# The last 512 queries' output in two parts: three pairs of heads early, the last pair at the end

## The chip, the core and the metric

The kernel runs on one NeuronCore of a Trainium2 chip. The metric is the device time of one execution in microseconds (us). The engines are TensorE (PE in the profile, PEld for its weight loads), VectorE (DVE), ScalarE (ACT), GpSimd (POOL) and SyncE (SP), which here only issues DMAs.

## What is computed

Four sequences (B = 4) of 1024 tokens with 256 channels go through four residual blocks: a linear recurrence, a sparse feed-forward block, attention, and the feed-forward block again. Two of them matter here.

```python
x = x + attention(layernorm(x))     # 8 heads of 64, softmax over 1024 keys, out @ Wo.T
x = x + ffn(layernorm(x))
# ffn, for each of two branches:
#   xc = grouped convolution of x;  mean and var of xc over ALL 4096 tokens
#   score = softmax(linear(gelu(normalised xc)));  the 32 largest of 256 are kept
```

The mean and variance run over all tokens of all sequences. The second feed-forward block can therefore not compute a single score before the attention output of the last token is in x and its convolution has been measured.

## The kernel before

Tokens are worked on in tiles of 128; x stays on the chip as 32 tiles. `heads` computes attention for one sequence: it loops over two halves of 512 queries (`nb`), four pairs of heads (`g`, PAIRS = 4) and four tiles of 128 queries (`q`). One such unit makes, for each of its two heads (`j`), the scores `sc` by four matmuls (L881), the negated maximum `nm` on VectorE (L885), and the exponentials `pr` on ScalarE (L889). The exponentials must be transposed, and there are two ways:

- by DMA (`by_dma`, q = 0 and 2): ScalarE casts `pr` to 16 bits (L892), GpSimd makes the remainder (L893), and SyncE issues a transposing DMA into `d` (L894);
- by TensorE (q = 1 and 3): eight transposes into PSUM (`ptp`, L900), copied out by VectorE and ScalarE (L903, L905).

`values_sum` then multiplies the transposed exponentials with the values (`pmo`, L925: 48 matmuls after a DMA, 32 after TensorE), puts the reciprocal sums in place with one transpose (L933), copies those on ScalarE (`rb`, L935) and multiplies on VectorE into `on` (L936). These sums are held back: the list `pending` holds units by TensorE and is taken from in the next unit, `late` holds units by DMA and is taken from in the next unit by DMA, and what is left follows after the loops.

`output` makes the projection of one query tile. It splits `on` (128 x 512: four pairs of 128) into a high part on ScalarE (`onp0`, L945) and a low part on GpSimd (`onp1`, L946), multiplies both with the split weights (`products`, three matmuls per pair, so twelve per tile into `pmy`, L170) and adds the result to x on VectorE (L948). `onp0` and `onp1` have one buffer each.

`f2.head` is the start of the second feed-forward block for two tiles of a block (its argument `pairs` says which two): layer norm on VectorE (L133 to L136, `rsqrt` being L55 to L66), normalisation on ScalarE (`xn`, L145), transposes (`pt`, L147), a copy (`ft`, L524), the convolution (`pc`, L529), an activation (`xc_f`, L533) and the statistics (`bst_f`, L534). When all statistics are there, `norm_scale` turns them into a scale, and the 32 tiles of the feed-forward block follow (`Ffn.tile`: maxima and replacements at L674, the subtraction of line 628, and so on).

`merge` interleaves all of this: `heads` is the main list of steps (STEPS = 64 per sequence), and each entry of `side` is (step at which it starts, generator, steps between its parts). A scheduler then orders each engine's queue by its own estimate of times. The queues are in order: an instruction that waits holds up all behind it on its engine. For the last sequence the output of the second half of queries starts a step before the end with two tiles, then comes the head of the feed-forward block for these, and after the merge the other two tiles and their head.

Of the kernel before, what the change touches and what calls it, by code (L numbers as in the profile page):

```python
# [10 lines left out]
F32 = mybir.dt.float32  # L11
I32 = mybir.dt.int32
F32R = mybir.dt.float32r
# [3 lines left out]
ALU = mybir.AluOpType  # L17
# [4 lines left out]
P = 128  # L22
B = 4
# [5 lines left out]
NBLK = B * T // 512  # L29
HEADS = 8  # L30
HD = 64
PAIRS = HEADS // 2
# [132 lines left out]
def products(nc, dst, pairs, start=True, stop=True):  # L165


    terms = [(x, y) for a, b in pairs for x, y in ((a[0], b[0]), (a[0], b[1]), (a[1], b[0]))]
    for i, (x, y) in enumerate(terms):
        nc.tensor.matmul(dst, x, y, start=start and i == 0, stop=stop and i == len(terms) - 1)  # L170


def by_block(v):

    return [
        v[b * T : (b + 1) * T, :].rearrange("(q p r) d -> r p q d", p=P, r=CH)[r] for b in range(B) for r in range(CH)
    ]
# [12 lines left out]
STEPS = 64  # L190
# [4 lines left out]
class Lru:  # L195
# [31 lines left out]
    def two(self, name):  # L227
        return [self.cp.tile([P, KD, D], F32R, tag=f"{name}{i}", name=f"{name}{i}") for i in range(2)]
# [544 lines left out]
class Attention:  # L773
# [82 lines left out]
    def heads(self, b, psum):  # L856

        nc, sp, wp = self.nc, self.sp, self.hp  # L860
        kh, kl, la, lb = self.k[b]
        late, pending = [], []
        for nb, g, q in ((nb, g, q) for nb in range(2) for g in range(PAIRS) for q in range(4)):
            by_dma = q % 2 == 0
            if g == 0:
                self.on[b, nb, q] = wp.tile([P, PAIRS, P], F32, tag=f"on{q}", name=f"on{q}")
            qs = self.qs[b, nb, g]
            ssum = sp.tile([P, 2], F32, tag="ssum", name="ssum", bufs=4)
            if by_dma:
                pts = [wp.tile([P, 2 * TPB, P], F16, tag=f"d{j}", name=f"d{j}", bufs=2) for j in range(2)]  # L870
                parts = ((0, lb[0]), (TPB, lb[0]), (0, lb[1]))
                terms = [(v[:, c, :], i + c) for c in range(TPB) for i, v in parts]
            else:
                pts = [wp.tile([P, TPB, P], F32, tag=f"p{j}", name=f"p{j}") for j in range(2)]
                terms = [(la[:, c, :], c) for c in range(TPB)]
            for j in range(2):
                sc = psum.tile([P, T], "sc", "sc")
                for i, kk in enumerate((kh, kl)):
                    for kb in range(2):
                        sl = slice(kb * 512, (kb + 1) * 512)  # L880
                        nc.tensor.matmul(  # L881
                            sc[:, sl], qs[:, j, q * P : (q + 1) * P], kk[:, sl], start=(i == 0), stop=(i == 1)
                        )
                nm = sp.tile([P, 1], F32, tag="nm", name="nm", bufs=4)
                nc.vector.tensor_reduce(nm, sc, AX.X, ALU.max, negate=True)  # L885
                if by_dma:
                    nc.vector.tensor_scalar(nm, nm, PSHIFT * math.log(2.0), None, ALU.add)  # L887
                pr = wp.tile([P, T], F32, tag="pr", name="pr", bufs=3)
                nc.scalar.activation(pr, sc, AF.Exp, bias=nm, accum_out=ssum[:, j : j + 1])  # L889
                if by_dma:  # L890
                    pd = wp.tile([P, 2, T], F16, tag="pd", name="pd", bufs=2)
                    nc.scalar.copy(pd[:, 0, :], pr)  # L892
                    nc.gpsimd.tensor_tensor(pd[:, 1, :], pr, pd[:, 0, :], ALU.subtract)  # L893
                    nc.sync.dma_start_transpose(pts[j], pd.rearrange("p i k -> p (i k)"))  # L894
                else:
                    for half in range(2):
                        pt = psum.tile([P, 4, P], "t", "ptp")
                        for kk in range(4):
                            kc = 4 * half + kk
                            nc.tensor.transpose(pt[:, kk, :], pr[:, kc * P : (kc + 1) * P], self.ident)  # L900
                        dst = pts[j][:, 4 * half : 4 * half + 4, :]
                        if half == 0 and b == B - 1:
                            nc.vector.tensor_copy(dst, pt)  # L903
                        else:
                            nc.scalar.copy(dst, pt)  # L905
                if j == 0 and pending:
                    self.values_sum(*pending.pop(0), psum)
                if j == 1 and late and by_dma:
                    self.values_sum(*late.pop(0), psum)
                yield  # L910
            (late if by_dma else pending).append((pts, terms, ssum, self.on[b, nb, q][:, g, :]))
        for args in late + pending:
            self.values_sum(*args, psum)
# [21 lines left out]
        nc.scalar.copy(rb, po[:, 1, :])  # L935
        nc.vector.tensor_tensor(on, po[:, 0, :], rb, ALU.mult)  # L936

    def output(self, b, nb, psum, tiles=range(4)):

        nc = self.nc  # L940
        for q in tiles:
            xt = self.x[b * TPB + nb * 4 + q]
            py = psum.tile([P, D], "s", "pmy")
            on = [self.hp.tile([P, PAIRS, P], F32R, tag=f"onp{i}", name=f"onp{i}") for i in range(2)]
            nc.scalar.copy(on[0], self.on[b, nb, q])  # L945
            nc.gpsimd.tensor_tensor(on[1], self.on[b, nb, q], on[0].bitcast(F32), ALU.subtract)  # L946
            products(nc, py, [([t[:, g, :] for t in on], [t[:, g, :] for t in self.wvo]) for g in range(PAIRS)])
            nc.vector.tensor_tensor(xt, xt, py, ALU.add)  # L948
            yield

# [23 lines left out]
def run(*gens):  # L974
    for g in gens:
        for _ in g:
            pass
# [51 lines left out]
def tile_kernel(ctx: ExitStack, tc: tile.TileContext, x_in, w_lru, vecs_in, rows, w_ffn, lin_t, w_attn, w_down, out):  # L1029
    nc = tc.nc  # L1030
# [31 lines left out]
    f2 = Ffn("f2", tc, bp, x, w)  # L1062

    with ExitStack() as c1:
        psum = Banks(c1.enter_context(tc.tile_pool(name="ps1", space=PSUM)), {"pu": 2, "po": 2, "py": 2, "pt": 2})
# [15 lines left out]
        for k in range(NBLK):  # L1081
            last = k >= NBLK - 2
# [10 lines left out]
            b = k // CH + 1  # L1093
# [24 lines left out]
    with ExitStack() as c2:  # L1118
        sp = c2.enter_context(tc.tile_pool(name="at_s", bufs=2))
        wp = c2.enter_context(tc.tile_pool(name="at_w", bufs=1))  # L1120
        two = lambda shape, name: [wp.tile(shape, F32R, tag=f"{name}{i}", name=f"{name}{i}") for i in range(2)]
        wqk, wvo, wd = two([P, KD, HEADS * HD], "wqk"), two([P, PAIRS, D], "wvo"), two([P, KD, P], "wd")
# [3 lines left out]
        at = Attention(tc, x, ident, ident64, wqk, wvo, wd, sp, wp)  # L1126
        with ExitStack() as c4:
            psum = Banks(
                c4.enter_context(tc.tile_pool(name="ps4", space=PSUM)), {"pl": 2, "px": 1, "pf": 2, "at": 3}
            )  # L1130
# [5 lines left out]
            with tc.issue_after(f1.gelu(1)):  # L1136
                for blk in range(2, NBLK):
                    g = f1.gelu(blk)
            with tc.issue_after(g):
                warm(nc, sp, AF.Exp)  # L1140
            tiles = [
                f1.tile(i, fp, psum, ("pl", "px", "pf"), fast=i == TPB - 1, tt=tts[i // 4]) for i in range(TPB)
            ]
# [24 lines left out]
        psum = Banks(c2.enter_context(tc.tile_pool(name="ps2", space=PSUM)), {"sc": 2, "t": 2, "s": 2})  # L1168
        at.hp = c2.enter_context(tc.tile_pool(name="at_h", bufs=1))
        fp = c2.enter_context(tc.tile_pool(name="f_s", bufs=2))  # L1170
        side = []
        for b in range(B):
            n = STEPS * b
            side += [
                (n + nb * 32 + 8 * g - 7, at.queries(b, nb, g, psum, "s"), 1)
                for nb in range(2)
                for g in range(PAIRS)
                if b or nb or g
            ]
            side.append((n + 33, at.output(b, 0, psum), 1.5))  # L1180
            side.append((n + STEPS - 1 if b == B - 1 else n + STEPS + 1.5, at.output(b, 1, psum, range(2 if b == B - 1 else 4)), 1 if b == B - 1 else 1.5))
            side.append((n + 40 if b == B - 1 else n + STEPS + 24, f2.head(2 * b, sp, psum, "s"), 2))
            last = b == B - 1
            side.append((n + STEPS if last else n + STEPS + 8, f2.head(2 * b + 1, sp, psum, "s", (0,) if last else (0, 1)), 1 if last else 2))
            if b < B - 1:
                side.append((n + 38, chain(at.prepare(b + 1, 0, psum, "s"), at.values(b + 1, 0, psum, "s")), 1.5))
                side.append((n + 56, chain(at.prepare(b + 1, 1, psum, "s"), at.values(b + 1, 1, psum, "s")), 1.5))
        side.append((1, at.values(0, 1, psum, "s"), 1))
        for i in range(TPB, NT):
            n = i - TPB  # L1190
            start = 1 + 6.75 * n if n < TPB else STEPS * (n // TPB) - STEPS + 48.25 + 8 * (n % TPB + 1)
            side.append((start, f1.tile(i, fp, psum, "sss", parts=wfs, fine=True), [1, 1, 1, 1, 1, 2, 1]))
        merge(chain(*(at.heads(b, psum) for b in range(B))), side)
        run(at.output(B - 1, 1, psum, range(2, 4)), f2.head(NBLK - 1, sp, psum, "s", (1,)))
    with ExitStack() as c3:
        psum = Banks(c3.enter_context(tc.tile_pool(name="ps3", space=PSUM)), {"pl": 2, "px": 3, "pf": 3})
        fp = c3.enter_context(tc.tile_pool(name="f_e", bufs=4))
# [5 lines left out]
        tiles = [f2.tile(i, fp, psum, ("pl", "px", "pf"), by_block(out), fast=i >= NT - 2) for i in range(NT)]  # L1203
# [98 lines left out]
```

## Time and profile before

| | us |
|---|---|
| median of 4 runs | 1535.94 |
| lowest and highest of the runs | 1532.78, 1540.67 |
| profiled execution | 1541.21 |
| its span, first to last instruction | 1539.5 |
| busy in the span: TensorE, VectorE, ScalarE, GpSimd | 1300.6, 1182.3, 1015.8, 682.2 |

In the profile's rows, a time stands first (start in us from the span's beginning, or a total), then the duration in us, the engine, the line, the operation and `out<-in`. `xN` means N instructions merged into one row; the bracket at the end tells how long the engine had been idle just before and what ended that. The windows view gives busy time of each engine in a stretch, with the number of instructions; PEclk is the share of the clock that TensorE was granted.

### The profile page before, as it was taken

How to read it: one execution, taken by the hardware profiler on the slowest of the kernel's cores; microseconds unless marked ns; L12 is line 12 of the kernel's file. 1: busy time of each engine (PE TensorE's matmuls, PEld its weight loads, DVE VectorE, ACT ScalarE, POOL GpSimd, SP SyncE). 2: the span in 40 equal slices, each digit the busy share in tenths (PEclk: the TensorE clock that was granted, in tenths of full speed). 3: DMA queues.
4: the chain of work that ended last, by engine and by line, in shares of the span. 5: the costliest groups of instructions: out<-in, count | busy, mean ns of one | idle time of the engine just before them, and what ended most of it. 6: DMA issues, size and time to landing. Idle time of an engine off the chain costs nothing. (4 is left out here: it accounts for less than half of the span.)

```text
span 1539.5 us, 28691 instructions
## 1 busy us (share of the span) xinstructions
PE 1300.6 (84%) x10134; PEld 963.8 (63%) x10136; DVE 1182.3 (77%) x3674; ACT 1015.8 (66%) x2145; POOL 682.2 (44%) x848
## 2 busy tenths in 40 slices
PE   5879998698898898888988989888999998656775
PEld 3535455365676766766776767677777776434454
DVE  8976665697878887878768687777676675499998
ACT  5353433664787877796777777877777776466664
POOL 2043423161545453544544544454344434057776
PEclk9999999698999999999999999999999999779898
DMA  3010000331454343334433444334444554000000
GB/s 117 32 41 14 21 21 14 134 105 41 76 97 89 63 76 73 73 73 82 81 73 60 71 78 82 64 61 82 71 82 80 87 95 85 1 11 27 22 25 28
DMA packets 288609, 96.51 MB, mean 63 GB/s; under 512 B 268233, under 2 KB 284626, under 8 KB 288466
## 3 DMA queue, kind: packets, MB, share of 16 engines
q1 hardware_dynamic: 283024, 88.50, 28.6%
q10 hardware_dynamic: 5442, 6.18, 1.2%
q8 instruction: 80, 1.31, 0.3%
q14 instruction: 63, 0.52, 0.1%
HBM read 16.01 MB, written 11.53 MB: 18 GB/s over the span
## 5 line engine op out<-in xcount | busy, mean ns | idle before, releaser
L893 POOL TENSOR_TENSOR pd<-pr,pd 128x1024 f16<-128x1024 f32 x128 | 273.5, 2142 | 256.3 <-ACT pd L892 196.7
L885 DVE TENSOR_REDUCE nm<-sc 128x1 f32<-128x1024 f32 x256 | 308.5, 1218 | 77.8 <-PE sc L881 76.1
L889 ACT ACTIVATE pr<-sc,nm 128x1024 f32<-128x1024 f32 x256 | 286.2, 1121 | 91.5 <-DVE nm L887 54.7
L881 PE MATMUL sc<-kh,qs 128*128 128x512 f32 x512 | 185.3, 440 | 28.1 <-ACT pr L889 20.4
L881 PE MATMUL sc<-kl,qs 128*128 128x512 f32 x512 | 161.6, 396 | 0.0
L674 DVE MATCH_REPLACE8 wk<-m,wk 128x256 f32<-128x256 f32 x384 | 160.6, 428 | 0.1
L674 DVE MAX8 m<-wk 128x8 f32<-128x256 f32 x384 | 155.3, 432 | 0.4
L905 ACT COPY p<-ptp 128x512 f32<-128x512 f32 x224 | 124.4, 591 | 45.5 <-PE ptp L900 37.2
L900 PE MATMUL ptp<-ident,pr 128*128 128x128 f32 x1024 | 141.2, 278 | 15.0 <-ACT pr L889 14.5
L925 PE MATMUL pmo<-p,la 128*64 128x128 f32 x2048 | 144.3, 290 | 5.3 <-ACT ft L524 2.9
L900 PEld LDWEIGHTS ptp<-ident,pr 128*128 128x128 f32 x1024 | 118.3, 142 | 36.9 <-ACT pr L889 24.3
L925 PEld LDWEIGHTS pmo<-p,la 128*64 128x64 f32 x2048 | 123.4, 145 | 23.7 <-ACT ft L524 5.1
L892 ACT CAST pd<-pr 128x1024 f16<-128x1024 f32 x128 | 133.3, 1055 | 4.6 <-DMA d<-pd 3.6
L881 PEld LDWEIGHTS sc<-kh,qs 128*128 128x128 f32 x512 | 85.8, 197 | 53.6 <-ACT pr L889 32.2
L881 PEld LDWEIGHTS sc<-kl,qs 128*128 128x128 f32 x512 | 96.9, 190 | 23.4 <-issue 1.4
L925 PE MATMUL pmo<-d,lb 128*64 128x128 f16 x3072 | 102.1, 221 | 8.2 <-DVE qs L853 2.5
L925 PEld LDWEIGHTS <-lb 128*64 128x64 f16 x3072 | 91.5, 111 | 25.9 <-issue 19.8
L628 POOL TENSOR_TENSOR ex<-ex,wk 128x512 f32<-128x512 f32 x61 | 77.8, 1275 | 51.6 <-DVE wk L674 42.7
L921 POOL COPY rows<-rs 128x128 f32<-128x128 f32 x128 | 36.6, 298 | 129.2 <-PE pmo L933 72.0
L936 DVE TENSOR_TENSOR on<-pmo,rb 128x128 f32<-128x128 f32 x128 | 36.5, 285 | 71.2 <-ACT rb L935 70.7
L147 PE MATMUL pt<-ident,xn 128*128 128x128 f32 x256 | 49.0, 313 | 42.4 <-ACT xn L145 30.6
L615 ACT ACTIVATE ex<-pl,nm 128x256 f32<-128x256 f32 x128 | 60.6, 474 | 35.1 <-POOL nm L613 34.3
(306 smaller groups left out, 2821.4 us busy)
## 6 DMA issues: line engine op xcount, KB each, us to landing
tt<-ft SPq DMA_DIRECT2D x16, 256.0 KB
tt<-tt SPq DMA_DIRECT2D x8, 512.0 KB
out<-x SPq DMA_DIRECT2D x32, 128.0 KB
x<-in_x ACTq DMA_DIRECT2D x6, 512.0 KB
pf<-pfs SPq DMA_DIRECT2D x12, 256.0 KB
full<-pf SPq DMA_DIRECT2D x24, 128.0 KB
d<-pd SPq DMA_TRANSPOSE x128
wa<-in_w_attn SPq DMA_DIRECT2D x2, 640.0 KB
```

Source lines behind the costliest of these rows:

```text
L147: nc.tensor.transpose(pt[:, k, i * P : (i + 1) * P], xn[:, k * P : (k + 1) * P], ident)
L615: nc.scalar.activation(ex[:, s, :], pl[:, s, :], AF.Exp, bias=nm[:, s : s + 1], accum_out=ssum[:, s : s + 1])
L628: pool.tensor_tensor(ex, ex, wk, ALU.subtract)
L674: ins = make(*args).ins
L881: nc.tensor.matmul(sc[:, sl], qs[:, j, q * P : (q + 1) * P], kk[:, sl], start=(i == 0), stop=(i == 1))
L885: nc.vector.tensor_reduce(nm, sc, AX.X, ALU.max, negate=True)
L889: nc.scalar.activation(pr, sc, AF.Exp, bias=nm, accum_out=ssum[:, j : j + 1])
L892: nc.scalar.copy(pd[:, 0, :], pr)
L893: nc.gpsimd.tensor_tensor(pd[:, 1, :], pr, pd[:, 0, :], ALU.subtract)
L900: nc.tensor.transpose(pt[:, kk, :], pr[:, kc * P : (kc + 1) * P], self.ident)
L905: nc.scalar.copy(dst, pt)
L925: nc.tensor.matmul(po[j * HD : (j + 1) * HD, 0, :], v, pts[j][:, c, :], start=(n == 0), stop=(n == len(terms) - 1),)
```

## The change

For the last sequence's second half of queries, and only there, four things differ. In the last pair of heads the units come in the order 0, 2, 1, 3, so both units by DMA precede both by TensorE, and their held-back sums are taken in the two units by TensorE. `output` gets a range of pairs: from step STEPS − 5.5 on it makes the first three pairs of all four tiles and adds them to x. After the merge, `output` makes the last pair alone, two tiles at a time, each two followed by their head of the feed-forward block. In these last calls (`fast`) the low part is made on VectorE in place of GpSimd.

```diff
-        for nb, g, q in ((nb, g, q) for nb in range(2) for g in range(PAIRS) for q in range(4)):
+        for nb, g, q in (
+            (nb, g, q)
+            for nb in range(2)
+            for g in range(PAIRS)
+            for q in ((0, 2, 1, 3) if b == B - 1 and nb and g == PAIRS - 1 else range(4))
+        ):
...
-                if j == 1 and late and by_dma:
+                if j == 1 and late and by_dma != (q > 0 and (b, nb, g) == (B - 1, 1, PAIRS - 1)):
                     self.values_sum(*late.pop(0), psum)
...
-    def output(self, b, nb, psum, tiles=range(4)):
+    def output(self, b, nb, psum, tiles=range(4), pairs=slice(0, PAIRS), fast=False):
         nc = self.nc
+        lower = nc.vector if fast else nc.gpsimd
         for q in tiles:
             xt = self.x[b * TPB + nb * 4 + q]
             py = psum.tile([P, D], "s", "pmy")
-            on = [self.hp.tile([P, PAIRS, P], F32R, tag=f"onp{i}", name=f"onp{i}") for i in range(2)]
-            nc.scalar.copy(on[0], self.on[b, nb, q])
-            nc.gpsimd.tensor_tensor(on[1], self.on[b, nb, q], on[0].bitcast(F32), ALU.subtract)
-            products(nc, py, [([t[:, g, :] for t in on], [t[:, g, :] for t in self.wvo]) for g in range(PAIRS)])
+            on = [self.hp.tile([P, PAIRS, P], F32R, tag=f"onp{i}", name=f"onp{i}")[:, pairs] for i in range(2)]
+            src, wvo = self.on[b, nb, q][:, pairs], [t[:, pairs] for t in self.wvo]
+            nc.scalar.copy(on[0], src)
+            lower.tensor_tensor(on[1], src, on[0].bitcast(F32), ALU.subtract)
+            products(
+                nc,
+                py,
+                [([t[:, g, :] for t in on], [t[:, g, :] for t in wvo]) for g in range(pairs.stop - pairs.start)],
+            )
             nc.vector.tensor_tensor(xt, xt, py, ALU.add)
             yield
...
-            side.append((n + STEPS - 1 if b == B - 1 else n + STEPS + 1.5, at.output(b, 1, psum, range(2 if b == B - 1 else 4)), 1 if b == B - 1 else 1.5))
+            if b < B - 1:
+                side.append((n + STEPS + 1.5, at.output(b, 1, psum), 1.5))
+            else:
+                side.append((n + STEPS - 5.5, at.output(b, 1, psum, pairs=slice(0, PAIRS - 1)), 1.5))
...
-            side.append((n + STEPS if last else n + STEPS + 8, f2.head(2 * b + 1, sp, psum, "s", (0,) if last else (0, 1)), 1 if last else 2))
+            if not last:
+                side.append((n + STEPS + 8, f2.head(2 * b + 1, sp, psum, "s"), 2))
...
-        run(at.output(B - 1, 1, psum, range(2, 4)), f2.head(NBLK - 1, sp, psum, "s", (1,)))
+        for j in range(2):
+            last = at.output(B - 1, 1, psum, range(2 * j, 2 * j + 2), slice(PAIRS - 1, PAIRS), True)
+            run(last, f2.head(NBLK - 1, sp, psum, "s", (j,)))
```

## The prediction

> **What bounds the kernel now.** I cut the end of the kernel into stages with the windows view.
>
> ```profile
> core 0: us, PE busy (x) PEld busy (x) DVE busy (x) ACT busy (x) POOL busy (x), PEclk, DMA share, GB/s
> 1287.00:1299.40 12.40, 10.52 (x121) 8.45 (x118) 6.99 (x13) 7.88 (x15) 4.90 (x5) 1.00 0.46 86
> 1299.40:1334.00 34.60, 21.86 (x173) 15.89 (x173) 14.43 (x47) 12.29 (x25) 9.74 (x9) 0.84 0.17 31
> 1345.00:1400.00 55.00, 35.79 (x131) 22.75 (x129) 54.21 (x232) 37.77 (x113) 35.67 (x59) 0.81 0.05 18
> ```
>
> While attention runs (first row) TensorE is the fullest engine, 10.52 of 12.40 us. In the second row nothing is full: that stretch is a chain of short steps, and the change works in it. In the last row VectorE is full; 32 tiles of top-k follow there, and they can't start before the batch statistics are complete. So the kernel's time is the moment of the last statistics plus a VectorE-bound tail. The waits of VectorE after 1334 us show how full the tail is:
>
> ```profile
> DVE m L674 <- PE pl L556: 4.0, 2, 3.0
> DVE x L662 <- PE pf L699: 3.0, 1, 3.0
> DVE wk L674 <- ACT e L618: 0.8, 1, 0.8
> ```
>
> 7.8 us of waits, 7.0 of them at its two ends. Then the timeline of the second row, cut to its chain:
>
> ```profile
> 1311.16 0.42 DVE L948 TENSOR_TENSOR x<-x,pmy 128x256 f32<-128x256 f32 x1 [3.37 <-PE pmy L170]
> ...
> 1313.08 1.27 POOL L946 TENSOR_TENSOR onp<-on,onp 128x512 fp32r<-128x512 f32 x1 [4.49 <-ACT onp L945]
> 1313.22 1.14 DVE L66 SCALAR_TENSOR_TENSOR norm_f<-fx_t,norm_f 128x2 f32<-128x2 f32 x1
> 1313.54 0.33 PE L933 MATMUL pmo<-ident,rows 128*128 128x128 f32 x1
> ...
> 1318.35 1.12 PE L529 MATMUL pc<-ft,cw 128*64 128x256 f32 x4 [0.68 <-ACT ft L524]
> 1319.40 2.93 PE L170 MATMUL pmy<-wvo,onp 128*128 128x256 f32 x12
> ...
> 1322.90 1.27 POOL L946 TENSOR_TENSOR onp<-on,onp 128x512 fp32r<-128x512 f32 x1 [8.56 <-ACT onp L945]
> 1324.23 1.46 PE L170 MATMUL pmy<-wvo,onp 128*128 128x256 f32 x10 [0.78 <-POOL onp L946]
> 1325.72 0.42 DVE L948 TENSOR_TENSOR x<-x,pmy 128x256 f32<-128x256 f32 x1 [2.25 <-PE pmy L170]
> ...
> 1333.53 0.43 DVE L534 BATCH_NORM_STATS2 bst_f<-xc_f 128x6 f32<-128x256 f32 x1 [4.34 <-ACT xc_f L533]
> ```
>
> Three marks: x of tiles 0 and 1 is complete at 1311.16+0.42 = 1311.58; x of tiles 2 and 3 at 1326.14; the last statistics end at 1333.96. The last head sum (L933) ends at 1313.87. So: end of statistics = first half complete + a gap of 14.56 + 7.82.
>
> **The change part by part.** I take the two built programs' queues, engine by engine. All queues are the same up to 1277.3 us, SyncE's queue throughout; the change does what it says. TensorE's matmul count stays (12 products per tile, now 9+3).
>
> *Added and removed work.* ScalarE: a 512-wide cast takes 0.62, a 128-wide copy 0.27 (L935); in a straight line between them a 384-wide one is 0.50, so a tile costs 0.77 for 0.62, 0.6 in all for four tiles. VectorE: four more adds of 0.42 and four subtractions of 0.29 (the 128-wide L936), 2.8 us; four of the adds lie in the head steps, where VectorE is 56% busy, the rest is on the path below. GpSimd: 1.27 becomes 0.95 (128-wide copy 0.29, same line), and the last quarter leaves it.
>
> *The last pair's stage.* The second unit by DMA now takes the place of the first unit by TensorE, and its scores enter TensorE at 1287.4 as those did. Steps from rows: scores of a head 0.93, eight transposes 1.2, a sum by TensorE 1.96+0.33, by DMA 1.5+0.33, nine products 1.3 (ten in 1.44), 4.7 from GpSimd's end of a split to the sum that needs its transpose (1303.64 to 1308.39). The walk down the new queues:
> - Both heads' scores end at 1289.2; products of tile 0 to 1290.5. The single hi buffer makes ScalarE's cast for tile 1 wait for those products, and the exponentials of the second DMA unit wait behind that cast and behind VectorE's maximum of the other head: they start at 1291.3 instead of 1289.9.
> - In TensorE's queue the first DMA unit's first sum matmul stands before tile 1's remaining products. Its transpose leaves GpSimd at 1287.6 and lands at 1292.3: TensorE waits some 1.2 us, with the next scores queued behind.
> - Scores of the first TensorE unit to 1295.1; sum of the first DMA unit to 1296.9; its transposes to 1298.5; the last unit's scores around tile 2's products, to 1301.35.
> - GpSimd subtracts tile 2's three pairs ahead of the last split for DMA, so that ends at 1299.95; its transpose lands at 1304.65 (before: 1308.39). Nobody waits for it: TensorE wants it at 1307.
> - From 1301.35 TensorE has no wait: 4+4 transposes and one matmul 1.26, nine products 1.3, eight transposes 1.2, a sum 2.23, 34 matmuls of the DMA sum 1.06, eight transposes 1.2, the rest of that sum 0.78, the last sum 2.29; together 11.3. The last sum ends at 1312.65, 1.2 us earlier than before.
>
> *First half.* Before, tiles 0 and 1 were ready ahead of the last sum. Now VectorE's queue has the last sum's multiply in front of tile 0's add: copy 0.27, multiply 0.29, add 0.42, subtraction 0.3, statistics 0.65, add 0.42: complete at 1315.0, 3.4 later than before. That is what the change gives back.
>
> *The gap.* Before: 7.89 from x complete to pc's end at 1319.47, and 6.67 for 12 products, cast, subtraction, ten products and add. In the second half the same head took 6.83 (1326.14 to 1332.97). Now the gap is one subtraction 0.3 + 6.83, then activation 0.53 and statistics 0.43 of the first half, add 0.42, subtraction 0.3, statistics 0.65, add 0.42: 9.9. The six remaining products hide beside these, even at the 0.24 each of the x12 row.
>
> Sum: 1315.0+9.9+7.8 = 1332.7 against 1333.96: 1.2 us earlier.
>
> One row and one rule belong here. L66 took 1.14 us at 1313.22, while GpSimd's subtraction ran; the next two took 0.16. Line 628 on VectorE took 1.25 beside a GpSimd add and 0.69 alone. The Trainium skill, "SBUF — State Buffer", section "SBUF: two separate sides", says that a VectorE operation with two SBUF inputs and a GpSimd one share a port pair under an exclusive lock and the loser waits for the whole instruction. This speaks against moving a subtraction of two SBUF operands to VectorE; by it each of the four could stand behind a GpSimd operation. In the new queue only the first meets one (a 0.29 copy, off the path); GpSimd's queue holds nothing after that, so the sum by rule and by rows is the same here, and 6.83 instead of 7.89 already holds the lock's absence.
>
> *The tail.* The change doesn't touch it, but its queues come out in another order. VectorE's work is the same: 256 maxima and 256 replacements. I gave every instruction of the new order the time of the old one in the same place of its queue: in three places VectorE would reach for an exponential (e8) before ScalarE has ended it, by 0.63, 0.32 and 0.15 us, two of them of one tile; before, the smallest margin was 0.11. Nothing there can be gained, as VectorE doesn't wait; the cost lies between 0 and about 1.1. I take 0.6.
>
> Total: −1.2+0.6 = −0.6. The profiled execution took 1541.21 (span 1539.5 and 1.71 around it), so it would take 1540.6. The median of the runs, 1535.94, is 5.3 below the profiled one; with the same step it becomes **1535.3**.
>
> **The rivals.**
> - *The first half goes ahead of the last sum (faster).* If tile 0's and 1's steps slip between the head sums, x of the first half is complete near 1309.5, as on1 is there at about 1307.5. Then pc ends at 1316.6, the second half is complete by 1319.4, the statistics end at 1327.2: 6.7 less, **1529.8** with 0.6 for the tail. For it: the products are short and their inputs ready. Against it: the queues are in order and the last multiply and the last sum stand in front. A milder form: TensorE never waits in the last pair's stage. Its work from 1287.4 is 23.8 us, the last sum would end at 1311.2, 1.5 better: 1533.8.
> - *VectorE starves in the tail (slower).* By the same laying-out, in six tiles GpSimd's negated maximum comes 0.42 to 1.04 us after ScalarE wants it, 4.4 in all; if all passes on to VectorE, with 0.95 from the e8's, the tail grows by 5.4: 5.4−1.2 = +4.2, **1540.1**. For it: margins were already down to 0.11. Against it: the median margin of an e8 was 2.2 us, ScalarE is 69% busy there and catches up. It is slower by over 0.5% only from 8.9 us of waits, 0.28 for each of 32 tiles.
> - *Transposes in a row queue up.* If the four of the last pair ran one behind the other at 4.7 each from 1287.6, the last would land at 1306.4, still before TensorE asks at 1307: no loss. Each 1 us beyond that is 1 us.
>
> **How the numbers follow.** Forecast 0.62, first half ahead or no waits 0.17, starving 0.17, others of either sign 0.04. The forecast's own range is 1533.0 to 1537.5, by the tail's bounds and a microsecond of error in a walk of 30 steps, and the runs shown lie between 1532.78 and 1540.67. To leave out no more than 2 in 10 the range reaches to the two first rivals: 1529.0 to 1540.8. A difference under 0.5%, 7.7 us, is about what a measurement of this kernel can't tell from none. Beyond it on the fast side lies half of the faster rival with some of the others, 0.10; on the slow side the tail's worst, 0.08.
>
> **What would show it.** Right: the last head sum ends near 1312.7; the first half's x is complete after it, near 1315; the two last pmy groups have six products, with 10 us between the halves instead of 14.6; statistics end near 1332.7; VectorE waits in the tail under 1.2 us more. Wrong: a first half complete before the last sum, TensorE waiting over 3 us between 1287 and 1301, or VectorE's waits in the tail over 10 us.

## The result and the profile after

The changed kernel takes 1533.04 us (median of 46 runs, 1527.89 to 1538.76), the kernel before 1536.88 (67 runs, 1532.01 to 1541.46): a ratio of 0.9978, 95% interval [0.9971, 0.9984]. By the ratio that is 3.4 us faster, a fifth of a per cent (the two medians lie 3.8 apart). It is a real gain, as the interval leaves out 1, but below the 0.5% that the prediction counted as no change. The median lies in the range and 2.3 us under the forecast. The forecast was counted from four runs of the kernel before, whose median was 0.94 lower than that of the 67, so the gain itself was missed by some 3 us: 0.6 was forecast.

The profiled execution after took 1535.25, its span is 1533.53. The span is 6.0 shorter than before, but not all of that is the change. I measure from a common point: the start of the last pair's first scores. TensorE's queue is the same in both kernels up to there (and every queue up to 2.1 us ahead of it), yet it came at 1279.41 before and at 1276.81 after, 2.60 earlier. From there on:

| us after the start of the last pair | before | after | predicted |
|---|---|---|---|
| last head sum ends | 34.46 | 31.92 | 33.24 |
| x of tiles 0, 1 complete (first half) | 32.17 | 33.98 | 35.59 |
| x of tiles 2, 3 complete (second half) | 46.73 | 43.45 | 45.5 |
| last statistics end (the stage) | 54.54 | 51.26 | 53.3 |
| tail, last statistics to end of span | 205.55 | 205.46 | 206.15 |

So of the 6.0 us, 2.6 lie ahead of the stage, 3.28 in it and 0.1 in the tail. In the stage the first half gives back 1.81 and the gap between the halves brings 5.09. A second profile of the changed kernel gave 51.26 for the stage again.

The windows view of the kernel after, for the same two stretches of the stage as before (moved by those 2.60) and for a stretch of the tail as far from the last statistics:

```profile
core 0: us, PE busy (x) PEld busy (x) DVE busy (x) ACT busy (x) POOL busy (x), PEclk, DMA share, GB/s
1284.40:1296.80 12.40, 11.53 (x113) 9.50 (x113) 7.38 (x15) 9.39 (x17) 8.65 (x7) 1.00 0.58 110
1296.80:1328.07 31.27, 20.12 (x186) 14.35 (x185) 15.21 (x53) 11.10 (x25) 2.35 (x7) 0.75 0.13 25
1339.11:1394.11 55.00, 37.72 (x124) 23.47 (x122) 53.28 (x230) 38.31 (x112) 33.57 (x56) 0.78 0.05 15
```

In the first row TensorE now does 11.53 us of work in 12.40, against 10.52: the early products fill its gaps. The second row, the chain of short steps, is 31.27 long where it was 34.60, and GpSimd's 9.74 us of busy time there have shrunk to 2.35. The tail is VectorE's, as before. The timeline of the kernel after, cut to the chain:

```profile
1308.40 0.33 PE L938 MATMUL pmo<-ident,rows 128*128 128x128 f32 x1
1308.49 0.60 PE L170 MATMUL pmy<-wvo,onp 128*128 128x256 f32 x3
...
1309.07 0.29 DVE L941 TENSOR_TENSOR on<-pmo,rb 128x128 f32<-128x128 f32 x1 [1.87 <-ACT rb L940]
1309.28 0.41 DVE L959 TENSOR_TENSOR x<-x,pmy 128x256 f32<-128x256 f32 x1
1309.51 0.82 PE L170 MATMUL pmy<-wvo,onp 128*128 128x256 f32 x3 [0.42 <-DVE on L941]
1309.61 0.28 DVE L953 TENSOR_TENSOR onp<-on,onp 128x128 fp32r<-128x128 f32 x1
1310.37 0.42 DVE L959 TENSOR_TENSOR x<-x,pmy 128x256 f32<-128x256 f32 x1
...
1316.45 1.12 PE L529 MATMUL pc<-ft,cw 128*64 128x256 f32 x4 [0.68 <-ACT ft L524]
1317.50 1.01 PE L170 MATMUL pmy<-wvo,onp 128*128 128x256 f32 x3
1318.13 0.43 DVE L534 BATCH_NORM_STATS2 bst_f<-xc_f 128x6 f32<-128x256 f32 x1 [4.22 <-ACT xc_f L533]
...
1319.84 0.42 DVE L959 TENSOR_TENSOR x<-x,pmy 128x256 f32<-128x256 f32 x1
...
1327.64 0.43 DVE L534 BATCH_NORM_STATS2 bst_f<-xc_f 128x6 f32<-128x256 f32 x1 [4.34 <-ACT xc_f L533]
```

The last head sum ends at 1308.73. The first half is complete only after it, at 1310.79: in TensorE's queue the three products of tile 0 stand behind the last sum (they start at 1308.49), and in VectorE's queue the last multiply (L941) stands in front of the adds. Then one head of the feed-forward block runs, the second half needs three products per tile, and it is complete at 1320.26: 9.47 behind the first, where it was 14.56. The way from there to the last statistics (7.81) is what it was.

### The profile page after: what moved, and what is told of

Read it like the earlier page. It is cut to its first block, busy times and chain, and to the rows that moved or that the text cites. A ratio compares the mean times of both kernels' runs of the same rounds, so it can differ in the third digit from the quotient of the medians.

```text
span 1533.5 us, 28721 instructions
## 1 busy us (share of the span) xinstructions
PE 1299.9 (85%) x10134; PEld 962.8 (63%) x10136; DVE 1184.4 (77%) x3682; ACT 1016.4 (66%) x2149; POOL 681.0 (44%) x848
## 3 DMA queue, kind: packets, MB, share of 16 engines
q8 instruction: 80, 1.31, 0.4%
HBM read 16.01 MB, written 11.53 MB: 18 GB/s over the span
## 5 line engine op out<-in xcount | busy, mean ns | idle before, releaser
L941 DVE TENSOR_TENSOR on<-pmo,rb 128x128 f32<-128x128 f32 x128 | 36.5, 285 | 66.0 <-ACT rb L940 65.3
L699 PE MATMUL pf<-wf,vt 128*128 128x256 f32 x288 | 84.0, 438 | 3.8 <-ACT vt L697 3.5
```

The source lines that it names most:

```text
L699: nc.tensor.matmul(dst, vt[:, k, :], w.wf[:, k, :], start=(k == 0 and bias is None), stop=(k == KD - 1))
```

## The experiments

Two theories share the 3.28 us. **A**: the split makes the gain, because the gap between the halves shrinks. **B**: the order of the units makes it, because the last head sum comes earlier. Marks are given as above, from the start of the last pair. The first four kernels ran on one chip (before: 1535.1 there), the other four on another (before: 1537.01).

**The order alone.**

```diff
 kernel before, with only
-        for nb, g, q in ((nb, g, q) for nb in range(2) for g in range(PAIRS) for q in range(4)):
+        for nb, g, q in (
+            (nb, g, q)
+            for nb in range(2)
+            for g in range(PAIRS)
+            for q in ((0, 2, 1, 3) if b == B - 1 and nb and g == PAIRS - 1 else range(4))
+        ):
...
-                if j == 1 and late and by_dma:
+                if j == 1 and late and by_dma != (q > 0 and (b, nb, g) == (B - 1, 1, PAIRS - 1)):
```

> The kernel before with one part of the change: the units of the last pair in the order 0, 2, 1, 3, and their sums taken as in the change; the output stays in one piece. I count from the start of the last pair's first scores to the end of the last statistics (54.55 us before, 51.26 after), and name two marks in it: the end of the last head sum (34.46 before, 31.92 after) and the gap between the two halves' completed x (14.56 before, 9.47 after). Theory A, the gain is made by splitting the output (shorter gap), and the order alone moves only the last sum: last sum near 32 to 33, gap still 13.5 to 15, the whole 53 to 55, ratio to before 0.999 to 1.0005. Theory B, the gain is the order's, because no transposing DMA is late any more: the whole 51 to 52, ratio 0.998.

Measured: 1534.65, ratio 1.0001 [0.9983, 1.002]. The last sum ended at 34.47 (before: 34.46), the first half at 32.78, the gap was 13.55, the stage 54.13. The last sum did not move at all, where 32 to 33 was expected. The timeline of this kernel's TensorE shows what stands in its way:

```profile
1286.10 0.74 PE L886 MATMUL sc<-kh,qs 128*128 128x512 f32 x2 [3.10 <-ACT pr L894]
...
1296.20 1.68 PE L170 MATMUL pmy<-wvo,onp 128*128 128x256 f32 x12
...
1303.44 0.33 PE L938 MATMUL pmo<-ident,rows 128*128 128x128 f32 x1
1303.52 1.68 PE L170 MATMUL pmy<-wvo,onp 128*128 128x256 f32 x12
1305.13 1.97 PE L930 MATMUL pmo<-p,la 128*64 128x128 f32 x32
1307.03 0.33 PE L938 MATMUL pmo<-ident,rows 128*128 128x128 f32 x1
```

Twelve products of one tile stand between the last two head sums: the last sum begins 1.61 us after they begin. And 3.10 us of idle time stand early in the stage, with nothing to fill them. In the kernel after the same places read:

```profile
1299.38 1.31 PE L170 MATMUL pmy<-wvo,onp 128*128 128x256 f32 x9
1300.53 1.03 PE L905 MATMUL ptp<-ident,pr 128*128 128x128 f32 x8
1301.49 1.96 PE L930 MATMUL pmo<-p,la 128*64 128x128 f32 x30
1303.38 0.33 PE L938 MATMUL pmo<-ident,rows 128*128 128x128 f32 x1
1303.64 1.14 PE L930 MATMUL pmo<-d,lb 128*64 128x128 f16 x34
1304.71 1.09 PE L905 MATMUL ptp<-ident,pr 128*128 128x128 f32 x8
...
1306.25 0.33 PE L938 MATMUL pmo<-ident,rows 128*128 128x128 f32 x1
1306.51 1.97 PE L930 MATMUL pmo<-p,la 128*64 128x128 f32 x32
```

No products between the sums, and nine instead of twelve ahead of them (1.15 from their start to that of the next instruction, where it was 1.52 for the twelve). These two places make 1.98; from the last unit's second scores to the end of the last sum the kernel after needs 11.58 and the order alone 13.37, 1.79 more.

**The split alone.**

```diff
 kernel after, with the old order
-        for nb, g, q in (
-            (nb, g, q)
-            for nb in range(2)
-            for g in range(PAIRS)
-            for q in ((0, 2, 1, 3) if b == B - 1 and nb and g == PAIRS - 1 else range(4))
-        ):
+        for nb, g, q in ((nb, g, q) for nb in range(2) for g in range(PAIRS) for q in range(4)):
...
-                if j == 1 and late and by_dma != (q > 0 and (b, nb, g) == (B - 1, 1, PAIRS - 1)):
+                if j == 1 and late and by_dma:
```

> The change without its order: units of the last pair in the order 0, 1, 2, 3 as before, output split in three pairs early and one pair at the end, the last low part on VectorE. Theory A: gap 9.3 to 10, the last sum no earlier than before (34 to 36, as the second unit by DMA ends late), the whole 52.5 to 54, ratio to before 0.9985 to 0.9995. Theory B: the last sum stays at 34.5 or more and the first half waits for it, the whole 54 or more, ratio 1.000.

Measured: 1532.82, ratio 0.9991 [0.9968, 1.0013]. Gap 9.48, as after. The last sum ended at 33.67 (34 to 36 was expected), the first half at 35.72, the stage at 53.01. In the old order the last transposing DMA is late for TensorE:

```profile
1298.24 0.83 PE L925 MATMUL pmo<-d,lb 128*64 128x128 f16 x23 [1.22 <-DMA d<-pd]
```

So the gap belongs to the split, as A has it. But neither part alone makes the stage what it is: the order takes 0.41 off it, the split 1.53, both 3.28. The last sum moved by 0.0, by 0.8, and by 2.5 with both. TensorE's idle time between the start of the last pair and the end of the last head sum, by the trace and its waits view, shows why:

| | before | order alone | split alone | after |
|---|---|---|---|---|
| products of the output in that stretch | 24 | 24 | 36 | 36 |
| TensorE idle, us | 5.27 | 5.55 | 3.06 | 1.43 |
| of that, waiting for exponentials | 3.6 | 4.1 | 1.3 | 0 |
| waiting for a transposing DMA | 1.5 | 1.4 | 1.8 | 0.8 |

The order alone moves the idle time about and takes none of it away. The split puts twelve more products into the stretch, where TensorE would have waited for exponentials. What is left then are waits for a late DMA and for exponentials, 3.1 us in all, and with the split in place the order brings them down to 0.8. With both, TensorE works 1.3 us more than before and is idle 3.8 less, which is the 2.5 of the last sum.

All this is the stage. From the start of the last pair to the end of the span the profiles take 260.09 before, 257.61 with the order alone, 259.68 with the split alone and 256.72 with both, as the tail was 2.06 shorter than before in the second and 1.13 longer in the third; no run shows why. Neither interval excludes no change in time; the reading rests on the marks of one profile each, and the order's 0.41 is no more than two profiles of one program can differ by (0.54, see the repeats).

**The engine of the low part.** In the last calls the 128-wide subtraction goes back to GpSimd.

```diff
-        lower = nc.vector if fast else nc.gpsimd
+        lower = nc.gpsimd
```

> The changed kernel with the last pair's low parts on GpSimd in place of VectorE. Theory A, the engine matters little, as a 128-wide GpSimd operation takes 0.29 and only hand-overs are added: the whole 51.3 to 52.3, ratio to before 0.998 to 0.9985. Rival: GpSimd's operations lock VectorE's small two-input steps (one took 1.14 in place of 0.16 before), which costs 1 us or more in each half: the whole 53 to 54.

Measured: 1533.85, ratio 0.9993 [0.9977, 1.0009]; stage 51.42, 0.16 later than after. The timeline of this kernel:

```profile
1286.71 0.24 PE L930 MATMUL pmo<-d,lb 128*64 128x128 f16 x1 [0.47 <-DMA d<-pd]
...
1307.87 0.45 POOL L953 TENSOR_TENSOR onp<-on,onp 128x128 fp32r<-128x128 f32 x1 [0.57 <-ACT onp L952]
...
1309.71 0.16 DVE L66 SCALAR_TENSOR_TENSOR norm_f<-fx_t,norm_f 128x2 f32<-128x2 f32 x1
```

GpSimd takes 0.45 for what VectorE does in 0.28 (L953 in the chain above), but that reaches none of the marks. The last head sum is already 0.18 later than in the kernel after (32.11), and that much is there 17.7 us after the start, ahead of the first of these subtractions at 25.0; a transposing DMA kept TensorE waiting 0.47 early in the stage, where it was 0.21. From the last sum to the first half it is 2.06 in both kernels, and the gap is 9.45 against 9.47. So the engine of the low part makes no difference here that can be seen. The small steps of L66 ran at 0.16 here too; the 1.14 seen before has not come back, and nothing of GpSimd's lay beside them. The Trainium skill, "SBUF — State Buffer", section "SBUF: two separate sides", says that of a VectorE operation with two SBUF inputs and a GpSimd one that reads SBUF, the one that comes second waits for the other's whole instruction. These calls did not put that to the test: no two such instructions met.

**The first half ahead of the last sum.** This is the prediction's faster rival, made on purpose: tiles 0 and 1 get their last pair, and their head of the feed-forward block, as entries of the side list, so that they lie between the head sums.

```diff
                 side.append((n + STEPS - 5.5, at.output(b, 1, psum, pairs=slice(0, PAIRS - 1)), 1.5))
+                side.append((n + STEPS - 1, at.output(b, 1, psum, range(2), slice(PAIRS - 1, PAIRS), True), 0.25))
+                side.append((n + STEPS - 0.4, f2.head(2 * b + 1, sp, psum, "s", (0,)), 1))
...
-        for j in range(2):
-            last = at.output(B - 1, 1, psum, range(2 * j, 2 * j + 2), slice(PAIRS - 1, PAIRS), True)
-            run(last, f2.head(NBLK - 1, sp, psum, "s", (j,)))
+        last = at.output(B - 1, 1, psum, range(2, 4), slice(PAIRS - 1, PAIRS), True)
+        run(last, f2.head(NBLK - 1, sp, psum, "s", (1,)))
```

> The changed kernel with the last pair's output of tiles 0 and 1 and the first step of their head put ahead of the last head sum in the list of steps. Theory A, the first half waits in queues for a sum it doesn't need: its x is complete at 30 to 31.5 (33.98 after, 32.17 before), the gap grows to 10 to 11.5, and the whole falls to 49 to 50.7, ratio to before 0.9965 to 0.9978. Rival: the first half's steps push the last sum and with it the second half back by as much: the whole 51 to 52, ratio 0.998.

Measured: 1529.92, ratio 0.9977 [0.9959, 0.9995]. Last sum 32.87, first half 30.92, gap 9.14, stage 47.86: 6.68 less than before, and shorter than expected (49 to 50.7), as the gap did not grow (10 to 11.5 was expected). The timeline:

```profile
1304.73 0.60 PE L170 MATMUL pmy<-wvo,onp 128*128 128x256 f32 x3
1305.57 0.41 DVE L959 TENSOR_TENSOR x<-x,pmy 128x256 f32<-128x256 f32 x1
1305.71 1.97 PE L930 MATMUL pmo<-p,la 128*64 128x128 f32 x32 [0.38 <-DVE on L941]
1307.61 0.33 PE L938 MATMUL pmo<-ident,rows 128*128 128x128 f32 x1
```

Three products of each of the two tiles slip in before the last sum (those of the second at 1304.73) and push it back by about a microsecond against the kernel after; the first half is complete at 1305.98, 1.95 before the last sum ends. The tail was 206.25 here, 0.8 longer than after, but 205.25 in a second profile of this program (below).

**The split with nothing early.** Old order; the products of the first three pairs are taken out of the side list and made at the end, per two tiles, ahead of the last pair's.

```diff
-                side.append((n + STEPS - 5.5, at.output(b, 1, psum, pairs=slice(0, PAIRS - 1)), 1.5))
+                pass
...
-            last = at.output(B - 1, 1, psum, range(2 * j, 2 * j + 2), slice(PAIRS - 1, PAIRS), True)
-            run(last, f2.head(NBLK - 1, sp, psum, "s", (j,)))
+            t = range(2 * j, 2 * j + 2)
+            run(at.output(B - 1, 1, psum, t, slice(0, PAIRS - 1)), at.output(B - 1, 1, psum, t, slice(PAIRS - 1, PAIRS), True))
+            run(f2.head(NBLK - 1, sp, psum, "s", (j,)))
```

> The change's split with nothing made early: old order of units, and at the end, for each two tiles, the first three pairs' part, then the last pair's part (VectorE low part), then their head. Theory A, what shortens the gap is that nine of twelve products, with their cast and subtraction, are out of it: here they are back, gap 13.5 to 15.5, the whole 54.5 to 57, ratio to before 1.000 to 1.002. Rival, that two small parts on two engines run better than one large part: gap 11 to 12.5, the whole 51.5 to 53.5, ratio 0.998 to 0.9995.

Measured: 1543.22, ratio 1.005 [1.0031, 1.0069]; gap 15.35, first half 39.37, stage 62.40, which is 5.4 us above the worst that I had allowed. The timeline after the last sum:

```profile
1305.98 0.33 PE L933 MATMUL pmo<-ident,rows 128*128 128x128 f32 x1
1307.05 1.33 PE L170 MATMUL pmy<-wvo,onp 128*128 128x256 f32 x9 [0.74 <-DVE on L936]
1308.87 0.50 PE L170 MATMUL pmy<-wvo,onp 128*128 128x256 f32 x2 [0.48 <-ACT onp L947]
1309.94 1.10 PE L170 MATMUL pmy<-wvo,onp 128*128 128x256 f32 x7 [0.58 <-POOL onp L948]
1311.37 2.27 PE L170 MATMUL pmy<-wvo,onp 128*128 128x256 f32 x6 [0.33 <-ACT onp L947]
```

All four splits and groups of two tiles now come in a row behind the last sum: the last sum is early (31.58, as no product is in its way), but the first half is complete 7.8 after it. I had counted too little of what stood beside the head sums before: there the whole output of tiles 0 and 1 lay ahead of the last sum (24 products, above), here nothing does. So this run is no measure of the split by itself against the kernel before. Against the split alone it differs only in when the first three pairs are made, and making them early is worth 9.4 us of the stage (62.40 against 53.01).

**The first half ahead, in the old order.** The fourth kernel's edit with the second kernel's order.

> The kernel with the first half ahead of the last sum, but with the units of the last pair in the old order 0, 1, 2, 3. If the order still matters, the last transposing DMA holds TensorE up (1.22 in the run with the split alone) and the last unit's scores come later: last sum 34 to 35 (32.87 with the new order), the whole 49 to 50.5 (47.86). Rival, the order is worth nothing once the first half goes ahead: the whole 47.5 to 48.5.

Measured: 1531.44, ratio 0.9967 [0.995, 0.9984]. Last sum 34.63, first half 31.83, stage 48.92, between the two expectations. The last transposing DMA was expected to hold TensorE up, and did not in this kernel; ahead of the last sums TensorE waited 0.72 us for an exponential and 0.57 for parts of `onp` instead. The order still brings the last sum 1.8 forward, but with the first half out of the way of the end only 0.5 to 1.1 of that is left in the stage (the repeat just below gives 48.40). In time no difference can be seen, and to the end of the span the old order even takes less: 253.37 from the start of the last pair.

**Repeats.** The changed kernel and the version with the first half ahead, unchanged, on the second chip.

> The changed kernel once more, to see how far the marks repeat: last sum 31.92, first half 33.98, gap 9.47, the whole 51.26, each within 0.3; the start of the last pair, which stood between 1269.7 and 1279.4 us in six runs whose queues are the same up to there, may fall anywhere in 1268 to 1281. Ratio to before 0.997 to 0.9985. If the whole moves by over 1 us, single profiles can't tell the parts apart.

> The version with the first half ahead once more, on one chip with the changed kernel: the whole 47.9 within 0.3, ratio to before 0.995 to 0.9965 if its 6.7 us in the stage reach the time, 0.9975 if the tail takes 3 us of them back.

Measured: the changed kernel 1531.89, ratio 0.9964 [0.995, 0.9977], stage 51.26 (all marks within 0.01; the ratio lies below what was expected); the version with the first half ahead 1529.47, ratio 0.9951 [0.9935, 0.9967], stage 48.40, tail 205.25. This stage is 0.54 longer than in the first profile of the same program, more than the 0.3 that was allowed. Nearly all of it (0.51) lies in the gap, where TensorE's transposes and convolution took longer. First profile, then second:

```profile
1309.97 0.93 PE L147 MATMUL pt<-ident,xn 128*128 128x128 f32 x4 [2.03 <-ACT xn L145]
1311.57 0.86 PE L529 MATMUL pc<-ft,cw 128*64 128x256 f32 x4 [0.68 <-ACT ft L524]
```

```profile
1306.47 1.18 PE L147 MATMUL pt<-ident,xn 128*128 128x128 f32 x4 [2.02 <-ACT xn L145]
1308.32 1.12 PE L529 MATMUL pc<-ft,cw 128*64 128x256 f32 x4 [0.67 <-ACT ft L524]
```

The granted clock was 1.00 and 0.71 beside these two rows in the first profile, 0.62 and 0.50 in the second: it fell earlier there.

From the start of the last pair to the end of the span the second takes 253.65 and 254.11 in its two profiles, the changed kernel 256.69 and 256.72, the kernel before 260.09. The version with the first half ahead has the lowest median on both chips. The intervals of the ratios overlap on the second chip, so its lead over the changed kernel, 2.6 to 3.1 us, stands on the traces.

## Why the prediction was right, and where its sizes were off

The direction, the mechanism and "within 0.5%" were right. The time by itself tests little of that, as the range held times on both sides of the kernel before, and the gain of 0.6 that was forecast is smaller than the errors of its terms; the marks are the test. The stage gained 3.28 where 1.2 was forecast, and the difference is three terms of the sum (1.32, 0.29 and 0.43).

- **The last sum: 1.2 earlier forecast, 2.54 measured.** This is the largest miss, 1.32. The walk down TensorE's queue held to within 0.1 for most of its way, and to 0.3 at its start (moved by 2.60: the scores of the last pair's second unit end at 1289.5 against 1289.2, products of tile 0 at 1290.57 against 1290.5, the sum of the first unit by DMA at 1296.86 against 1296.9). The DMA landed 0.47 earlier than assumed and the last unit's scores ended at 1300.83 instead of 1301.35. The rest is the last stretch, "together 11.3", which took 10.50. Its eight terms came out 0.66 shorter, and they overlap the scores ahead of them by 0.16. Most of the 0.66 is the price of eight transposes, 1.2 taken twice (0.42); the nine products make 0.15, the two sums by TensorE 0.15. Durations of rows had been added, and for the transposes more than a duration, but on a busy TensorE the next instruction starts before a row ends. The kernel after shows it above: the nine products have a duration of 1.31, and the transposes behind them start 1.15 later; those eight have 1.03 and are followed after 0.96, the next eight 1.09 and 1.02; the last sum's 32 matmuls have 1.97 and its transpose starts after 1.89.
- **The first half: 2.35 behind the last sum forecast, 2.06 measured.** The queue order that causes it was right, though TensorE's products behind the last sum belong to the cause as much as VectorE's multiply. The steps were again added by their durations, and here too a row starts before the one ahead of it ends: the add at 1309.28, the multiply's end at 1309.36.
- **The gap: 9.9 forecast, 9.47 measured.** Its composition was right: one head and three products per tile. The last six products hid beside the activation and the statistics but for some 0.1 us, though they were slow: three at 1317.50 took 1.01, while three right behind the last sum, at 1308.49, took 0.60. The windows view puts the granted clock at 0.50 from 1317.40 to 1318.60 and at 1.00 from 1308.40 to 1309.10.
- **The end, 7.82:** measured 7.81.
- **The tail: 0.6 longer forecast, 0.1 shorter measured.** "Nothing there can be gained" was wrong. VectorE's waits in the tail of the kernel after:

```profile
DVE m L674 <- PE pl L556: 4.0, 2, 3.0
DVE x L662 <- PE pf L699: 1.7, 2, 1.3
DVE wk L674 <- POOL ob L651: 0.9, 1, 0.9
DVE wk L674 <- ACT e L618: 0.8, 1, 0.8
```

A new wait of 0.9 has come. The row puts it down to GpSimd, but the instruction that waits loads an exponential (`e`), and ScalarE ended that one just ahead of it:

```profile
1364.23 0.30 ACT L618 ACTIVATE e<-m,nm 128x8 f32<-128x8 f32 x1
...
1364.63 0.09 DVE L674 MATCH_VALUE_LOAD wk<-e,ex 128x8 f32 x1 [0.93 <-POOL ob L651]
```

So it is very likely the late exponentials of one tile, forecast at 0.63 and 0.32. But the wait at the very end (L662) fell from 3.0 to 1.7, which the forecast had left out. Over all ten profiles the tail lies between 203.25 and 206.67. The two profiles of the changed kernel differ by 0.03 in it, but the two of the version with the first half ahead by 1.00 (206.25 and 205.25), so the 0.1 between before and after says nothing. What sets the tail stays open; no edit here was made to choose it.

**The rivals.** The first half going ahead did not come about in this kernel, for the reason given (the queues are in order). Where it was made to, its price of 6.7 in the stage was met: 6.68 and 6.14. Its milder form, the last sum at 1311.2, was closer to the truth than the forecast (1311.33), but by luck: it has TensorE never waiting, and TensorE waited 0.54 for a cast and 0.21 for a DMA there, which made up for work priced too high by row durations. VectorE did not starve in the tail: its waits there add up to 7.4, against 7.8 before. The transposes did not hold up the last sum; in the old order, one did, by 1.22.

## What to carry to other kernels

A tail that waits for the last of something is shortened by what can be made of it before the last part is there, if the early work fills time in which an engine would wait: the same split with nothing made early took 9.4 us more in the stage. Two changes in one queue can need each other, so that each alone shows little; test them apart and together. A wait is put down to the engine that came last by the profile; what the waiting instruction reads tells whether that can be. In a walk down a busy queue add the distances from start to start, not the durations of rows.

## What the runs showed that I had not expected

Most of the scatter of the times comes from ahead of the changed stage. In ten profiles, of programs in which TensorE has the same queue up to there, the last pair began between 1269.65 and 1279.41: nearly 10 us. Behind it, the marks of the stage of two profiles of the changed kernel agree within 0.01. So a change of 3 us in 1536 can be read from one profile by marks counted from a common point, while a comparison of two spans, 6.0 us here, would have nearly doubled it. The version with the first half ahead repeats less well, 47.86 and 48.40, because the granted clock fell earlier in one of its profiles; a difference of half a microsecond between two kernels needs a look at the clock first.
